# A graph network's last result tiles: the work of the last quarter's results put on other engines, with a region of its own for each tile

## The chip, the cores and the metric

The kernel runs on one core of one Trainium2 chip. The metric is the device time of an execution in microseconds. A core has five engines with instruction streams of their own: TensorE (PE; its weight loads are listed as PEld), VectorE (DVE), ScalarE (ACT), GpSimd (POOL) and SyncE (SP), which in this kernel mostly issues DMA transfers. They wait for each other on semaphores. SBUF is the memory of 128 partitions on the core, PSUM the memory that TensorE writes its products to.

## What is computed

Two layers on 3327 nodes with 256 features, each added to its input. Layer 0 does two steps of a normalised adjacency product beside a sparse attention of its own (not touched here). Layer 1 is a graph attention with four heads. Cut to what matters:

```python
h = jnp.maximum(_layernorm(x, axis=-1), 0.0)
x = x + layer0(h, adj, ...)              # below: x1; it ends in a layer norm, times ln_g, plus ln_b
h = jnp.maximum(_layernorm(x, axis=-1), 0.0)
x = x + layer1(h, adj, W, a)

def layer1(h, adj, W, a):
    hp = (h @ W).reshape(n, H, FH)       # H = 4 heads of FH = 64
    s = jnp.einsum('nhf,hf->hn', hp, a_src)
    d = jnp.einsum('nhf,hf->hn', hp, a_dst)
    e = jax.nn.leaky_relu(s[:, :, None] + d[:, None, :], ALPHA)
    e = jnp.where(adj[None, :, :] > 0, e, -jnp.inf)
    attn = jax.nn.softmax(e, axis=2)
    out = jnp.einsum('hij,jhf->ihf', attn, hp).reshape(n, H * FH)
    return jax.nn.elu(out)
```

With r for a row of `out`, elu(r) is max(r, 0) + min(exp(r), 1) - 1, so the result is max(r, 0) + min(exp(r), 1) + x1 - 1.

## The kernel before

All work is cut into pieces. `plan.put(engine, length, rank, fn, needs=..., take=..., give=..., lag=..., hold=...)` records one piece: `length` is the author's estimate of its duration, `rank` its priority, `needs` the pieces it comes after, `take` and `give` the buffers it uses up and gives back. `Plan.order` plays the pieces through with these estimates and so fixes the order in which each engine's instructions stand; what each instruction really waits for follows from the tiles that it reads and writes. A changed estimate or a new piece anywhere can therefore move instructions elsewhere.

The program's phases: a preparation, 26 row blocks of layer 0's step 0, 26 of step 1 (both with TensorE as the busiest engine), and layer 1's attention over the neighbours, `attend_neighbours`, in four quarters `b` of W = 832 columns of rows (the last one has 831 that count). In a quarter, for each of 26 blocks `j` of neighbours, SP loads two pieces of the adjacency matrix (`at`, L1570, four buffers), ACT makes a mask of them (L1580, L1581), DVE makes the masked exponents of four heads (`exponents`, L1592, from an operand `both`, which lies in the space of `qq` for quarters 0 and 2 and in that of `c` for 1 and 3, into one of four `e` buffers or three others), and TensorE multiplies (`product`, L1608; `sums`, L1622, the softmax's denominators). At a quarter's end ACT copies numerators and denominators from PSUM to a tile `ot` of the kind `e` (`leave`, L1668 and L1671).

Then come the quarter's results, in seven tiles of 128 rows (the last of 64, or 63 in the last quarter):

- `fetch` (SP, L1683): x1 of these rows from DRAM (`x1s`) to `f`, three buffers;
- `turn` (PE, L1689): three transposes into `px`, a PSUM tile with two buffers: two of numerators, one of denominators;
- `invert` (DVE, L1693): the reciprocals of four denominators, to `mv`;
- `elu` (ACT, L1701): for each of four heads Relu and Exp over 64 columns, with the reciprocal as scale, from `px` to `ystage`, two buffers; it gives `px` back;
- `add` (DVE, L1705, L1706): min(exp, 1) + relu, then - 1 + x1;
- `store` (SP, L1709): 128 KB to DRAM; it gives `ystage` back when it has landed.

In quarters 0 to 2 these pieces stand among the next quarter's work; in the last quarter nothing but a verdict follows. The verdict (L1785 to L1799: two transposes of one column, two reductions of 128 values, one operation to `again`) says whether a general version has to run after all; each engine reads `again` (L1806) and branches past that version.

Other lines that matter: `layer1_loads` (L717 to L720) loads `ln_g`, `ln_b` and weights into `late` in step 0; `add_b` (L1278, POOL) adds `ln_b` to x for each row in step 1, and the sum goes into x1, which `x1s` holds; `late["b"]` is used nowhere else. `step` (L923 to L953) is GpSimd's search for a threshold in layer 0.

Of the kernel before, what the change touches and what calls it, by code (L numbers as in the profile page):

```python
# [10 lines left out]
F32 = mybir.dt.float32  # L11
# [3 lines left out]
AF = mybir.ActivationFunctionType  # L15
ALU = mybir.AluOpType
# [3 lines left out]
P = 128  # L20
N = 3327
NT = 26
NP = NT * P
D = 256
DA = 64
H = 4
FH = 64
# [543 lines left out]
def fast(  # L571
# [17 lines left out]
    nc = tc.nc  # L589
    V, S, T, GP = nc.vector, nc.scalar, nc.tensor, nc.gpsimd  # L590
# [10 lines left out]
    x1s = spill.tile([NT, P, D], F32, name="x1s")  # L601
# [29 lines left out]
    with ExitStack() as l0:  # L631
        wpool = l0.enter_context(tc.tile_pool(name="wpool", bufs=1))
        small = l0.enter_context(tc.tile_pool(name="small", bufs=2))
        epool = l0.enter_context(tc.tile_pool(name="epool", bufs=4))
# [823 lines left out]
        def attend_neighbours(rows, ends, done, fulls):  # L1458


            W = NP // 4
# [4 lines left out]
            extra = {}  # L1466
# [25 lines left out]
            def spread_heads(t0, t1):  # L1492

                held = {}

                def turn():
                    held["ps"] = ps_x.tile([(t1 - t0) * H, P], F32, name="px")
                    T.transpose(held["ps"], sd[:, 0, t0:t1, :].rearrange("p t h -> p (t h)"), ident)

                def exps():  # L1500
                    held["rows"] = small.tile([7 * H, P], F32, name="rows", bufs=1)[: (t1 - t0) * H]
                    S.activation(held["rows"], held["ps"], AF.Exp, scale=1.0 - ALPHA)

                def store():
                    for t in range(t0, t1):
                        nc.sync.dma_start(
                            highs[:, t * P : (t + 1) * P], held["rows"][(t - t0) * H : (t - t0 + 1) * H, :]
                        )

                rank = min(30.0 + t1, 59.0)  # L1510
                a = plan.put("PE", 0.12, rank, turn, needs=[z[0] for z in ends[t0:t1]], take=["px"])
                a = plan.put("ACT", 0.3, rank, exps, needs=[a], take=["rows"], give=["px"])
                return plan.put("SP", 1.0, rank, store, needs=[a], give=["rows"], lag=3.0)
# [4 lines left out]
            def broadcast(b, rank):  # L1518
# [11 lines left out]
                    got.append(plan.put("SP", 0.1, rank, fetch, needs=[after], lag=7.0 + 5.0 * a))  # L1530
                return got

            used_heads = [None, None]
            evacuated = None
            both = broadcast(0, 59.5)
            for b in range(4):
# [140 lines left out]
                for x0 in range(0, W, P):  # L1677
                    m = min(P, W - x0, N - lo - x0)
                    held = {}

                    def fetch(m=m, at=lo + x0, held=held):
                        held["x1"] = small.tile([P, H * FH + 2 * H], F32, name="f", bufs=BUFS["f"])[:, :D]
                        nc.sync.dma_start(held["x1"][:m], x1s.rearrange("t p d -> (t p) d")[at : at + m, :])  # L1683

                    def turn(m=m, x0=x0, q=q, held=held):
                        held["pr"] = ps_x.tile([P, 3, P], F32, name="px")
                        ot = q["ot"].rearrange("p k c w -> p k (c w)")
                        for k in range(3):
                            T.transpose(held["pr"][:m, k, :], ot[:, k, x0 : x0 + m], ident)  # L1689

                    def invert(m=m, held=held):
                        held["rec"] = small.tile([P, 4], F32, name="mv", bufs=BUFS["mv"])
                        V.reciprocal(held["rec"][:m], held["pr"][:m, 2, ::32])  # L1693

                    def elu(m=m, held=held):
                        y = held["y"] = small.tile([P, 2, D], F32, name="ystage", bufs=BUFS["ystage"])
                        pr = held["pr"][:m, :2, :].rearrange("p a b -> p (a b)")
                        for k in range(H):
                            part = slice(k * FH, (k + 1) * FH)
                            for a, fn in enumerate((AF.Relu, AF.Exp)):  # L1700
                                S.activation(y[:m, a, part], pr[:, part], fn, scale=held["rec"][:m, k : k + 1])  # L1701

                    def add(m=m, held=held):
                        y = held["y"]
                        V.scalar_tensor_tensor(y[:m, 0], y[:m, 1], 1.0, y[:m, 0], ALU.min, ALU.add)  # L1705
                        V.scalar_tensor_tensor(y[:m, 0], y[:m, 0], -1.0, held["x1"][:m], ALU.add, ALU.add)  # L1706

                    def store(m=m, at=lo + x0, held=held):
                        nc.sync.dma_start(out[at : at + m, :], held["y"][:m, 0])  # L1709

                    touched = [ends[t][1] for t in range((lo + x0) // P, min(NT - 1, (lo + x0 + m - 1) // P) + 1)]
                    f_ = plan.put("SP", 0.1, r1, fetch, needs=[touched, [a for a, _ in ends]], take=["f"], lag=3.0)
                    a = plan.put(
                        "PE", 0.4, r1 + 0.02, turn, needs=[out_of], take=["px"], give=["e"] * (x0 + P >= W)
                    )
                    a = plan.put("DVE", 0.2, r1, invert, needs=[a], take=["mv"])
                    a = plan.put("ACT", 2.0, r1, elu, needs=[a], take=["ystage"], give=["px", "mv"])
                    a = plan.put("DVE", 1.0, r1, add, needs=[a, f_], give=["f"], hold=0.9)
                    plan.put("SP", 0.1, r1, store, needs=[a], give=["ystage"], lag=2.5)

# [13 lines left out]
        for n in range(STEPS):  # L1734
            base = 30.0 * n
            scaled = plan.put(
                "DVE", 0.2, base - 50.0,
                lambda: V.tensor_scalar(gk[:, : DA + 1], gk[:, : DA + 1], 1.0 / (NT // 2 * P), None, ALU.mult), needs=[sums],
            )
            cuts = (0, 3, NT // 2, NT)  # L1740
            of = {}
            for k in range(3):
                p = stats(cuts[k], cuts[k + 1], base + (-50.0, -2.35, 0.0)[k], [keys, fresh], scaled)
                of.update(dict.fromkeys(range(cuts[k], cuts[k + 1]), p))
            if n == 0:
                guessed[0] = [*{id(p): p for p in of.values()}.values()]
            rows = [Row(n, i) for i in range(NT)]
            found = [search(r, base + r.i, keys, of[r.i], fresh) for r in rows]
            if n == 0:
                drawn[0] = rows[-1].pieces["logits"]  # L1750
            fulls = [
                full(n, t, (min(1.0 + 1.15 * t, 27.0) if n == 0 else base + 1.0 + t), [p[0] for p in sources], [p[1] for p in sources] if n == 0 else loaded[0])
                for t in range(NT)
            ]
            done = [attention(r, base + r.i, *found[r.i], right) for r in rows]
            failed.append(plan.put("DVE", 2.2, base + NT, failures, n, needs=[[a for a, _ in found]]))
            if n == 0:
                ends = [finish1(r, done[r.i], base + r.i + 0.2) for r in rows]
                stored = [y for _, _, y in ends]
                fetched = plan.put(  # L1760
                    "SP", 0.3, base + NT, fetch_keys, needs=[drawn[0], [k for k, _, _ in ends[: LAST + 1]]], lag=5.0
                )
                keys, sums = [fetched] + [k for k, _, _ in ends], [g for _, g, _ in ends]

                right, after = [], [done, stored]
                for lo in range(0, NT, 4):
                    hi = min(lo + 4, NT)
                    right.append(plan.put("SP", 0.1, base + NT, fetch_rhs, lo, hi, needs=after, lag=7.0))
                    after = [plan.put("POOL", 0.02, -90.0, lambda: None, needs=right[-1:], lag=0.0)]
                fresh = failed + [r.pieces["guess"] for r in rows]  # L1770
                used, sources = sources, [(p,) for p in fulls]

                def layer1():
                    late["g"], late["b"], late["wa"], late["a"] = layer1_loads()

                a = plan.put("SP", 0.5, base + 4.0, layer1, needs=[used, done[3]], take=["et"], lag=8.0)
                layer1_ready = plan.put(
                    "DVE", 3.7, base + 5.0, lambda: layer1_scores(late["wa"], late["a"]), needs=[a], take=["et"],
                    give=["et", "et"],
                )  # L1780
            else:
                ends = [finish2(r, done[r.i], fulls[r.i], base + r.i + 0.2) for r in rows]
        attend_neighbours(rows, ends, done, fulls)
# [62 lines left out]
```

## Time and profile before

| | us |
|---|---|
| median of 3 runs | 2241.94 (2241.08 to 2243.65) |
| the profiled execution | 2240.52 |
| its span, first to last instruction | 2238.6 |
| PE busy | 2177.3 |
| DVE busy | 1615.0 |
| ACT busy | 1455.7 |
| POOL busy | 925.1 |

The span is what the profile divides; the profiled execution's own time is 1.9 us longer. Busy times of the engines overlap. In the stretch from 2216.5 to the end, 22.1 us, PE is busy for 5.4, ACT for 12.4, DVE for 7.6 and POOL for 0.

### The profile page before, as it was taken

The page shows a single profiled execution, that of the slowest core. Times are in us where ns is not written, and L with a number is a line of the kernel's source. Part 1 is how long each engine was busy: PE and PEld are TensorE (multiplying, and loading weights), DVE is VectorE, ACT ScalarE, POOL GpSimd, SP SyncE. Part 2 cuts the span into 40 slices and gives each one's busy share as a digit, 9 for nine tenths or more (in the row PEclk, how much of TensorE's full clock was granted, in tenths as well). Part 3 has the DMA queues.
Part 4 walks back from the last instruction along what each step waited for, and adds up shares of the span by engine and source line. Part 5 has one row for each costly group of instructions (what it writes and reads, how often), then busy time and mean ns, then how long its engine had stood idle before and what let it go on. Part 6 is the DMA issues. An engine that isn't in the chain of part 4 may idle for free.

```text
span 2238.6 us, 36037 instructions
## 1 busy us (share of the span) xinstructions
PE 2177.3 (97%) x11978; PEld 1537.8 (69%) x11978; DVE 1615.0 (72%) x4229; ACT 1455.7 (65%) x2795; POOL 925.1 (41%) x2214
## 2 busy tenths in 40 slices
PE   7999999999999999999999999999999999999997
PEld 5487778777887778877878887887887433333332
DVE  5576657546655744178979877888777998989895
ACT  5776686566566652478887877878774455464653
POOL 6455355435544541256656666566653200000000
PEclk9999999999999999999999999999999999999998
DMA  3012221212212222621212222222225344444341
GB/s 99 20 38 70 68 70 54 70 49 64 70 53 70 70 83 67 191 76 56 76 49 70 59 74 72 81 62 66 69 75 154 121 129 137 116 144 119 102 128 42
DMA packets 192036, 183.76 MB, mean 82 GB/s; under 512 B 15354, under 2 KB 146144, under 8 KB 191712
## 3 DMA queue, kind: packets, MB, share of 16 engines
q1 hardware_dynamic: 189856, 180.10, 27.6%
q8 instruction: 96, 1.57, 0.3%
q10 hardware_dynamic: 1984, 1.26, 0.2%
q14 instruction: 100, 0.82, 0.1%
HBM read 164.41 MB, written 15.94 MB: 81 GB/s over the span
## 4 chain that ended last, share of the span: by engine, by line
PE 75%; ACT 8%; POOL 6%; DVE 5%; issue 3%; DMA 1%; SPq 0%; ACTq 0%; POOLq 0%; DVEq 0%
PE acca L1042 20%; PE accf L1074 20%; PE pl L1608 12%; PE px L1030 6%; PE pl L856 6%; ACT junk L907 5%; PE acca L1622 3%; PE accf L1622 3%; PE px L1217 2%; POOL sc L920 1%; PE px L1312 1%; PE px L1169 1%; DVE cands L967 1%; DVE y L962 1%; ACT et L1035 1%
## 5 line engine op out<-in xcount | busy, mean ns | idle before, releaser
L1042 PE MATMUL acca<-rhs,et 128*128 128x256 f32 x2704 | 619.4, 380 | 1.0 <-ACT et L1035 0.9
L907 ACT ACTIVATE junk<-e,sc 128x3327 fp8e5<-128x3327 f32 x182 | 559.2, 3073 | 48.1 <-POOL sc L952 46.8
L1042 PEld LDWEIGHTS acca<-rhs,et 128*128 128x128 f32 x2704 | 499.9, 191 | 64.4 <-ACT et L1035 2.9
L1074 PE MATMUL accf<-c,at 128*128 128x256 f32 x1352 | 313.5, 382 | 5.5 <-ACT f L1081 5.5
L1074 PE MATMUL accf<-main,at 128*128 128x257 f32 x1352 | 312.0, 382 | 5.6 <-DMA at<-in_adjt_dram 5.3
L962 DVE SCALAR_TENSOR_TENSOR y<-e,sc 128x1664 f32<-128x1664 f32 x104 | 209.0, 2010 | 149.0 <-POOL sc L949 147.0
L1074 PEld LDWEIGHTS accf<-main,at 128*128 128x128 f32 x1352 | 252.8, 191 | 47.9 <-issue 6.5
L1074 PEld LDWEIGHTS accf<-c,at 128*128 128x128 f32 x1352 | 250.0, 190 | 47.7 <-ACT f L1081 10.3
L1035 ACT COPY et<-px 128x512 f32<-128x512 f32 (+1 forms) x364 | 192.7, 553 | 136.1 <-PE acca L1042 72.9
L967 DVE MAX8 cands<-y 128x8 f32<-128x208 f32 x832 | 242.6, 361 | 3.6
L1017 DVE SCALAR_TENSOR_TENSOR e<-e,thr 128x832 f32<-128x832 f32 x208 | 213.1, 1082 | 2.2 <-DVE thr L1012 0.5
L870 ACT ACTIVATE e<-pl 128x1024 f32<-128x1024 f32 x208 | 179.0, 864 | 37.7 <-PE pl L856 37.5
L1581 ACT ACTIVATE et<-at 128x448 bf16<-128x448 f32 (+1 forms) x204 | 112.2, 550 | 137.3 <-DVE e L1592 81.5
L1030 PE MATMUL px<-ident,e 128*128 128x128 f32 x1352 | 191.2, 275 | 9.2 <-DVE gk L766 4.5
L1030 PEld LDWEIGHTS px<-ident,e 128*128 128x128 f32 x1352 | 159.5, 141 | 51.8 <-issue 15.3
L1608 PE MATMUL pl<-e,main 128*64 128x416 f32 x1024 | 187.2, 515 | 0.0
L856 PE MATMUL pl<-kt,qq 64*128 64x512 f32 (+1 forms) x832 | 173.5, 535 | 0.0
L1608 PEld LDWEIGHTS pl<-e,main 128*64 128x64 f32 x1024 | 71.0, 137 | 107.3 <-issue 92.0
L1592 DVE SCALAR_TENSOR_TENSOR e<-c,low,et 128x832 f32<-128x832 f32 x128 | 128.6, 1072 | 8.2 <-PE accf L1622 3.9
L856 PEld LDWEIGHTS pl<-kt,qq 64*128 64x128 f32 x832 | 71.6, 186 | 82.1 <-issue 75.7
L1592 DVE SCALAR_TENSOR_TENSOR e<-qq,low,et 128x832 f32<-128x832 f32 x120 | 120.5, 1074 | 2.6 <-ACT e L1668 2.0
L1580 ACT ACTIVATE at<-at 128x448 f32<-128x448 f32 (+1 forms) x204 | 109.8, 538 | 11.9 <-DMA at<-in_adjt_dram 11.8
(507 smaller groups left out, 2987.3 us busy)
## 6 DMA issues: line engine op xcount, KB each, us to landing
at<-in_adjt_dram SPq DMA_DIRECT2D x414, 256.0 KB
at<-in_adjt_dram SPq DMA_DIRECT2D x102, 192.0 KB
at<-in_adjt_dram SPq DMA_DIRECT2D x52, 128.0 KB
ys<-ystage SPq DMA_DIRECT2D x26, 256.0 KB
rhs<-in_x_dram SPq DMA_DIRECT2D x26, 128.0 KB
ystage<-in_x_dram SPq DMA_DIRECT2D x26, 128.0 KB
base<-ys SPq DMA_DIRECT2D x26, 128.0 KB
x1s<-ystage SPq DMA_DIRECT2D x26, 128.0 KB
```

The lines of the kernel that those rows point to most:

```text
L856: T.matmul(pl[:, r, :m], qq[half, self.i, :], kt[half, 512 * k : 512 * k + m], start=True, stop=True,)
L870: S.activation(self.e[:, 1024 * k : 1024 * k + 2 * w].rearrange("p (r w) -> p r w", r=2), pl, AF.Exp, accum_out=(self.p0, self.p1, self.p2 ...
L907: S.activation(junk[:, :N], self.e[:, :N], fn, bias=t, scale=-1.0, accum_out=dst, saturate=False)
L962: V.scalar_tensor_tensor(self.y[:, : hi - lo], self.e[:, lo:hi], self.up, self.e[:, lo:hi], ALU.is_lt, ALU.mult, accum_out=(self.h0, self. ...
L967: V.max(self.cands[:, o // PIECE, :], self.y[:, o - lo : min(o + PIECE, hi) - lo])
L1017: V.scalar_tensor_tensor(piece, piece, self.thr[:, o : o + 1], piece, ALU.is_gt, ALU.mult)
L1030: T.transpose(pt[:, k, :], self.e[:, j * P : (j + 1) * P], ident)
L1035: S.copy(self.et[g][:, :m, :], self.pt.pop(g)[:, :m, :])
L1042: T.matmul(self.acc, et[:, j - 4 * g, :], rhs[self.n][:, j, :], start=(j == 0), stop=(j == NT - 1))
L1074: T.matmul(self.acc[:, : self.w], self.at[j // JC][:, j % JC, :], self.src[:, j, : self.w], start=(j == 0), stop=(j == NT - 1),)
L1592: V.scalar_tensor_tensor(held["e"][:, k, :], extra["both"][b % 2][:, k, :], low[:, j, k : k + 1], held["mask"], ALU.max, ALU.mult,)
L1608: T.matmul(q["acc"][a][k * FH : (k + 1) * FH, c, :C], main[:, j, h * FH : (h + 1) * FH], held["e"][:, h, c * C : (c + 1) * C], start=(j == 0),
```

## The change

The last quarter's results (b = 3) get pieces of their own; the other quarters keep theirs, but for one operation. Since all quarters share `x1s`, the "- 1" moves into it: `ln_b` becomes `ln_b - 1` once, by GpSimd, after it was loaded, so that `x1s` holds x1 - 1. (A layer norm of x1 - 1 is that of x1.)

- `fetch_all` (SP): x1 - 1 for four tiles at once into the space of `qq`, after quarter 2's last exponents (`used_heads[0]`), and for the other three into a buffer of the kind `e`, after the last quarter's last exponents. Each tile has 768 columns there: three parts of 256.
- `quotient` (DVE): the reciprocals, into columns of a tile `rows`, then one product of 256 columns from PSUM, with the reciprocal of each head repeated 64 times, to part 1. It gives `px` back.
- `parts` (ACT): Relu of part 1 to part 0, Exp of part 1 in place, 256 columns each.
- `add_x1` (POOL): part 2 (x1 - 1) plus part 0.
- `join` (DVE): min(part 1, 1) + part 2, to part 0.
- `store` (SP): as before, from part 0; no buffer is given back.

```diff
@@ spread_heads
-                    held["rows"] = small.tile([7 * H, P], F32, name="rows", bufs=1)[: (t1 - t0) * H]
+                    held["rows"] = small.tile([P, P], F32, name="rows", bufs=1)[: (t1 - t0) * H]
@@ attend_neighbours
+            last, f_ = {}, None
...
                     def add(m=m, held=held):
                         y = held["y"]
                         V.scalar_tensor_tensor(y[:m, 0], y[:m, 1], 1.0, y[:m, 0], ALU.min, ALU.add)
-                        V.scalar_tensor_tensor(y[:m, 0], y[:m, 0], -1.0, held["x1"][:m], ALU.add, ALU.add)
+                        V.tensor_add(y[:m, 0], y[:m, 0], held["x1"][:m])
+
+                    def fetch_all(x0=x0, lo=lo):
+                        if x0 == 0:
+                            last["rec"] = small.tile([P, P], F32, name="rows", bufs=1)
+                        y = extra["both"][0] if x0 == 0 else epool.tile([P, NP], F32, name="e").rearrange(
+                            "p (k w) -> p k w", k=4
+                        )
+                        for k in range(4):
+                            x = x0 + k * P
+                            n = min(P, W - x, N - lo - x)
+                            if n > 0:
+                                last[x] = y[:, k, : 3 * D].rearrange("p (a d) -> p a d", a=3)
+                                nc.sync.dma_start(
+                                    last[x][:n, 2], x1s.rearrange("t p d -> (t p) d")[lo + x : lo + x + n, :]
+                                )
+
+                    def quotient(m=m, held=held, x0=x0):
+                        y, held["rec"] = last[x0], last["rec"][:, x0 // P * H : (x0 // P + 1) * H]
+                        held["y"] = y
+                        V.reciprocal(held["rec"][:m], held["pr"][:m, 2, ::32])
+                        V.tensor_tensor(
+                            y[:m, 1].rearrange("p (h f) -> p h f", h=H),
+                            held["pr"][:m, :2, :].rearrange("p a (h f) -> p (a h) f", h=2),
+                            held["rec"][:m].unsqueeze(2).to_broadcast([m, H, FH]),
+                            ALU.mult,
+                        )
+
+                    def parts(m=m, held=held):
+                        y = held["y"]
+                        S.activation(y[:m, 0], y[:m, 1], AF.Relu)
+                        S.activation(y[:m, 1], y[:m, 1], AF.Exp)
+
+                    def add_x1(m=m, held=held):
+                        GP.tensor_add(held["y"][:m, 2], held["y"][:m, 2], held["y"][:m, 0])
+
+                    def join(m=m, held=held):
+                        y = held["y"]
+                        V.scalar_tensor_tensor(y[:m, 0], y[:m, 1], 1.0, y[:m, 2], ALU.min, ALU.add)
...
-                    f_ = plan.put("SP", 0.1, r1, fetch, needs=[touched, [a for a, _ in ends]], take=["f"], lag=3.0)
+                    if b < 3:
+                        f_ = plan.put("SP", 0.1, r1, fetch, needs=[touched, [a for a, _ in ends]], take=["f"], lag=3.0)
+                    elif x0 % (4 * P) == 0:
+                        f_ = plan.put("SP", 0.4, r1, fetch_all, needs=[used_heads[0] if x0 == 0 else [last_e, f_], touched], take=["e"] * (x0 > 0), lag=4.0)
                     a = plan.put(
                         "PE", 0.4, r1 + 0.02, turn, needs=[out_of], take=["px"], give=["e"] * (x0 + P >= W)
                     )
+                    if b == 3:
+                        a = plan.put("DVE", 0.65, r1, quotient, needs=[a, f_], give=["px"])
+                        a = plan.put("ACT", 0.8, r1, parts, needs=[a])
+                        z_ = plan.put("POOL", 0.8, r1, add_x1, needs=[a, f_])
+                        a = plan.put("DVE", 0.45, r1, join, needs=[z_], hold=0.4)
+                        plan.put("SP", 0.1, r1, store, needs=[a], lag=2.5)
+                        continue
@@ fast, step 0
                 def layer1():
                     late["g"], late["b"], late["wa"], late["a"] = layer1_loads()
+                    late["less"] = lambda: GP.tensor_scalar(late["b"], late["b"], -1.0, None, ALU.add)
...
+                less = plan.put("POOL", 0.6, base + 5.0, lambda: late["less"](), needs=[a])
...
+                layer1_ready = [layer1_ready, less]
```

## Prediction

> **What bounds the kernel now.** The page first: its engine table says that TensorE fills the span and that no other engine does.
>
> ```profile
> PE 2177.3 (97%) x11978; PEld 1537.8 (69%) x11978; DVE 1615.0 (72%) x4229; ACT 1455.7 (65%) x2795; POOL 925.1 (41%) x2214
> ```
>
> So work taken from ACT or DVE is worth nothing where TensorE is busy beside it. The 40 slices give PE 9 everywhere but at the start and in the last one. The end is therefore read by itself. The chain of waits, asked for 2216 us to the end, leaves TensorE at 2217.06:
>
> ```profile
> 2216.57 0.49 PE px L1689 x3
> 2217.06 0.02 issue
> 2217.08 0.19 DVE mv L1693
> 2217.28 0.02 issue
> 2217.30 1.75 ACT ystage L1701 x8
> 2219.05 0.02 issue
> 2219.08 0.43 DVE ystage L1705
> 2219.51 0.02 issue
> 2219.53 0.43 DVE ystage L1706
> 2219.97 0.02 issue
> 2219.99 0.02 SPq L1709
> 2220.00 0.03 issue
> 2220.03 1.73 DMA out_dram<-ystage
> ...
> 2233.13 0.42 DVE ystage L1706
> ```
>
> The columns are start, length, who. Seven result tiles run one after the other from 2217.06 to 2233.55: 16.5 us with TensorE nearly idle. A tile is a transpose, a reciprocal, eight ACT operations over 64 columns, two DVE additions and a store; because `ystage` has two buffers, ACT also waits for a store to land (1.73 us, twice). The groups of lines for the same stretch say that ACT is the engine of it:
>
> ```profile
> L1701 ACT ACTIVATE ystage<-px,mv 128x64 f32<-128x64 f32 (+1 forms) x56 | 11.8, 337 | 3.7 <-DMA out_dram<-ystage 2.3 <-DVE ystage L1706 1.2 <-DVE mv L1693 0.2
> ```
>
> Last, the line that reads the verdict (L1806) shows what stands after the last result:
>
> ```profile
> L1806 SPq TENSOR_LOAD <-again x1: 683/683/683, 2231.5 to 2231.5; - x1
> L1806 SPq COMPARE_BRANCH  x1: 50/50/50, 2234.0 to 2234.0; - x1
> L1806 SPq EVENT_SEMAPHORE  x8: 17/17/17, 2236.7 to 2237.2; - x8
> ```
>
> SP branches 0.46 us after the last addition, its next instruction comes 2.6 us later, and the closing waits end at 2238.6: 5.05 us behind the last addition. The verdict itself was read earlier, at 2231.5, beside ACT's work.
>
> **What the Trainium skill says.** "ScalarE: Activation LUTs", section "What ACT_TABLE_LOAD costs": an operation with immediate scale and bias takes 186 ns + 0.833 ns per column, each pointer operand adds about 93 ns. This trace agrees: L1580 (no pointer, 416 columns in the mean) takes 538 ns against 533. For 256 columns that is 0.40 us. "SBUF — State Buffer", section "SBUF: two separate sides": a DVE operation with two SBUF inputs and a GpSimd operation exclude each other, the later one is blocked. The trace agrees: at 143.7 the add L1225 (POOL, 0.72) started just ahead of a DVE L962, which then took 2.40 instead of 1.95; at 349.96 the add came second, took 2.03, and ended 0.59 after L962. So an add holds up a DVE operation by some 0.5 us. "TensorE: Matmul & The Clock Gate", section "What's actually happening": an idle array falls to half clock after some 3.4 us. The trace agrees: three transposes take 0.55 at 2220.73 and 0.90 at 2223.67.
>
> **The change, part by part.** Steps of the last quarter's seven tiles:
>
> *Removed:* 56 ACT operations, 11.8 us busy, and ACT's 2.3 us of waits for stores (every tile has its own region now). *In their place:* 14 ACT operations of 256 columns. L1580's 384 columns take 0.51 and 448 take 0.56 to 0.58, which makes 0.38 to 0.40 at 256; I take 0.39, so Relu and Exp with the wait between them are 0.81 a tile. Upper end: L1298, 256 columns with pointer operands, 0.60.
>
> *DVE:* a reciprocal (0.18, L1693), then the product out of PSUM with a broadcast operand, not in this trace. Nearest rows: L1323, the same product from SBUF, 0.42, and L1173, a copy out of PSUM of that size, 0.42. I take 0.45, bounds 0.42 and 0.50. It reads one operand from SBUF, so I let it not contend with GpSimd. The join is one operation of L1705's kind, 0.42, where two stood.
>
> *GpSimd:* the add of 128x256, 0.72 (L1225, L1278). Bounds: 0.72 alone, 1.3 each time it meets a join.
>
> *TensorE:* a tile waits for its `px` buffer, which is now given back by the product instead of by eight ACT operations: 0.53 a tile (0.90 cold). It falls behind other work, as DVE is slower.
>
> The built order of DVE is quotients 0 to 3, join 0, quotients 4 and 5, join 1, quotient 6 (with the first verdict reduction inside), joins 2 to 6, then the second verdict reduction and `again`. DVE alone: 7 x (0.18 + 0.03 + 0.45) + 7 x 0.42 + 0.28 = 7.84, less 0.08 at each of some 15 places where the next operation does not depend on the last one (L1705 follows L1706 after 0.34) = 6.6. Now the waits, walked through by hand with these durations: product 0 ends 2217.74, Relu 2218.17, Exp 2218.59, add 2218.94; tile 3: product 2219.56, Exp 2220.78, add 2221.49, join 2223.82; tile 6: product 2222.53, Exp 2223.38, add 2224.40, join 2225.45. DVE loses 0.1 for `px` and 1.6 at joins behind adds: 2217.08 + 6.6 + 1.7 = 2225.4. Without the port's exclusion the last join ends 2224.2; with cold transposes 2226.05; with adds of 1.0 everywhere 2226.3; with ACT at 0.60 2226.5; all of these together 2226.9.
>
> *The end:* `again` was ready at 2231.46, 1.7 us before the last addition began; now it stands behind the last join. Reduction and final operation take 0.4 (0.28 + 0.15, L1798 and L1799, the first overlapping), the read 0.69, register work and branch 0.4: SP branches 1.5 after the last join instead of 0.46. The rest, 2.63 + 1.9 us, is as before, so the end stands 6.1 behind the join instead of 5.05. The seven stores (0.35 each on SP) go out before, at the joins' pace.
>
> Span: 2225.45 + 6.1 = 2231.55, that is 7.05 less.
>
> *Moved and added elsewhere, costed at nothing:*
> - Loads of x1. Four go to the space of the exponents' first operand (`qq`) when quarter 2 has read it last. In SP's order they stand ahead of the `at` loads issued at 2083.09, 2084.06, 2087.07 and 2088.04, and wait for DVE until 2086.37. SP is then held from 2080.4 to 2086.4 and issues four loads (0.43 each, L1683): the next `at` load goes out at 2088.1, 5 us late, lands some 3 us later (an estimate: 128 KB, L1709, take 1.73, and this is 256 KB), and ACT wants it at 2098.18 (L1580). Margin 7 us. The last three wait for the `e` buffer of row 21, free at 2207.9, and have until 2221.
> - GpSimd's b - 1, 128x256, at most 0.72, in row 5 of step 0: it stands behind L953 (ends 223.37), and the next GpSimd instruction begins at 226.34 after 2.74 us of waiting for ACT. Its loads have landed at 219.2. Without that cover it would cost 0.7 in one row's search.
> - The planner's order moves two matmuls and one `at` load around 250 us past three small DMAs: that load goes out at 254.8 instead of 252.2, wanted at 259.9; beyond that margin TensorE would wait as long as it is late.
> - In quarters 0 to 2 an addition replaces L1706: 0.42 (L1090) for 0.42.
>
> **Time.** The profiled execution took 2240.52 with a span of 2238.6. 7.05 less is 2233.5 there; the median of the runs is 2241.94, so 2234.9.
>
> **Rivals.** *GpSimd becomes the bound of the end.* For it: seven adds of 0.72 and seven joins of 0.42 that exclude each other, and GpSimd's times are rough. If every add takes 1.3 plus 0.1 of wake-up, the last ends 2218.2 + 9.8 = 2228.0, the join 2228.5, the span 2234.6: 4.0 less, 2237.9. Against: only adds 3 to 6 meet joins. *The closing part grows.* All five engines now branch within 1 us of each other, where four did it 1.7 us ahead; TensorE's branch shows 3.39 already. With 2 us more: 5 less, 2236.9. *A larger gain:* port exclusion not felt, product at 0.42: 2233.5. *Slower:* SP's queue. The fetch of x1 is parked ahead of the `at` loads; if its wait ended not at 2086.4 but with the next DVE result that is counted, late masks would reach ACT, DVE and TensorE. From 2093 on each microsecond costs one, and from 2100 on it eats the whole gain; held until 2105, it makes 2247. Against: the operand's last reader is quarter 2's last exponent, ended at 2086.37. That the change doesn't do what it says is excluded by the built order.
>
> **How the numbers follow.** Forecast 0.76, a larger gain 0.04, the closing part 0.08 (all three faster), GpSimd as the bound 0.09 (inside 0.2%), SP 0.03 (slower). 0.2% is 4.5 us, so "same" is 2237.5 to 2246.4. The likeliest one's own bounds, 2224.2 to 2226.9 for the last join, are 2233.7 to 2236.4; the three runs lie 2.6 us apart, so some 0.8 on each side, and upward to part of the rivals: 2233.0 to 2237.3.
>
> **What would show it.** In the profile after: last join at 2225 to 2226; ACT's two operations 0.39 each; adds of 0.72 for tiles 0 to 2 and over 1 later; joins of 0.42 to 0.9; SP's branch 1.5 behind the last join; no change in TensorE's time of entering the transposes (2216.5). Wrong would be: transposes later than 2217.5 (a cost in the quarters), or products above 0.6.

## The result, and the profile after

| us | before | after | repeat of after |
|---|---|---|---|
| median (range), runs | 2241.11 (2239.72 to 2243.65), 8 | 2235.27 (2233.45 to 2236.41), 8 | 2234.09 (2232.20 to 2235.23), 5 |
| ratio to before, 95% interval | | 0.9974 (0.9965 to 0.9983) | 0.9964 (0.9951 to 0.9978) |
| span of the profiled execution | 2238.6 | 2234.2 | 2233.1 |
| TensorE enters the last transposes | 2216.5 | 2218.7 | 2217.3 |
| from there to the end of the last result on DVE | 17.05 | 8.56 | 8.56 |
| from there to the end of the span | 5.07 | 6.96 | 7.20 |

The kernel became faster, by 5.8 us in the runs made right after the prediction and by 7.15 in the repeat (each against before timed beside it, hence the two ratios). The last two rows are called the join time and the end part below; together they are "the tail": 22.1 before, 15.5 and 15.8 after. The tail is the better measure of the change than the time: TensorE's entry into it differs by 1.4 us between two traces of before and by 1.3 between two of after.

The chain of waits after, from the first result on (columns: start, length, who):

```profile
2220.41 0.73 POOL qq L1742
2221.14 0.02 issue
2221.16 0.73 POOL qq L1742
...
2222.72 0.69 POOL qq L1742
2223.41 0.02 issue
2223.43 0.74 POOL e L1742
2224.16 0.11 issue
2224.27 1.66 POOL e L1742
...
2226.81 0.41 DVE e L1746
2227.22 0.21 DVE verdict L1852
2227.43 0.02 issue
2227.45 0.15 DVE again L1853
```

ACT, which carried this chain before, is gone from it. GpSimd's additions stand in its place, one behind the other with at most 0.11 us between them, and `again` stands last. The groups of lines of the same stretch, by shape (columns: tiles and shapes, count, busy us, mean ns, idle before):

```profile
L1742 POOL TENSOR_TENSOR qq<-qq 128x256 f32<-128x256 f32 x4 | 3.0, 756 | 453.7 <-ACT qq L1738 453.7
L1742 POOL TENSOR_TENSOR e<-e 128x256 f32<-128x256 f32 x2 | 2.5, 1266 | 0.0
L1746 DVE SCALAR_TENSOR_TENSOR qq<-qq 128x256 f32<-128x256 f32 x4 | 1.8, 459 | 0.0
L1729 DVE TENSOR_TENSOR qq<-px,rows 128x256 f32<-128x256 f32 x4 | 1.7, 424 | 0.1
L1739 ACT ACTIVATE qq<-qq 128x256 f32<-128x256 f32 x4 | 1.7, 417 | 0.1
L1738 ACT ACTIVATE qq<-qq 128x256 f32<-128x256 f32 x4 | 1.6, 405 | 0.6 <-DVE qq L1729 0.6
```

The wide operations cost what their nearest rows gave. The additions of the tiles in `e` don't: 1.27 in the mean of two, one of them 1.65. The line that reads the verdict shows the rest. Before, the four engines that the prediction doesn't show branched so (columns: count, shortest, median and longest in ns, first and last start):

```profile
L1806 ACTq COMPARE_BRANCH  x1: 54/54/54, 2232.2 to 2232.2; - x1
L1806 POOLq COMPARE_BRANCH  x1: 45/45/45, 2232.3 to 2232.3; - x1
L1806 PEldq COMPARE_BRANCH  x1: 3390/3390/3390, 2232.3 to 2232.3; - x1
L1806 DVEq COMPARE_BRANCH  x1: 76/76/76, 2233.8 to 2233.8; - x1
```

After:

```profile
L1860 SPq EVENT_SEMAPHORE  x8: 17/17/17, 2232.3 to 2232.8; - x8
...
L1860 SPq TENSOR_LOAD <-again x1: 784/784/784, 2227.7 to 2227.7; - x1
L1860 ACTq COMPARE_BRANCH  x1: 54/54/54, 2228.2 to 2228.2; - x1
L1860 POOLq COMPARE_BRANCH  x1: 45/45/45, 2228.2 to 2228.2; - x1
L1860 PEldq COMPARE_BRANCH  x1: 3427/3427/3427, 2228.3 to 2228.3; - x1
L1860 DVEq COMPARE_BRANCH  x1: 76/76/76, 2228.3 to 2228.3; - x1
...
L1860 SPq COMPARE_BRANCH  x1: 50/50/50, 2228.9 to 2228.9; - x1
```

The last join ended at 2227.22. SP branches 1.65 behind it (0.46 before), and its next instruction comes 3.38 later (2.68 before). All five engines branch within 0.7 us, where ACT, POOL and PE were 1.7 us ahead of SP before.

### The profile page after: what moved, and what is told of

The parts are those of the page before. It is cut to its first block, busy times and chain, and to the rows that moved or that the text cites. A ratio compares the mean times of both kernels' runs of the same rounds, so it can differ in the third digit from the quotient of the medians.

```text
span 2234.2 us, 35999 instructions
## 1 busy us (share of the span) xinstructions
PE 2177.5 (97%) x11978; PEld 1538.1 (69%) x11978; DVE 1614.5 (72%) x4229; ACT 1449.4 (65%) x2753; POOL 931.5 (42%) x2222
## 3 DMA queue, kind: packets, MB, share of 16 engines
q8 instruction: 96, 1.57, 0.3%
## 4 chain that ended last, share of the span: by engine, by line
PE 69%; issue 9%; ACT 9%; POOL 6%; DVE 5%; DMA 2%; SPq 0%; POOLq 0%; DVEq 0%; ACTq 0%
PE acca L1042 20%; PE accf L1074 19%; PE pl L1609 9%; ACT junk L907 6%; PE px L1030 6%; PE pl L856 5%; PE acca L1623 2%; PE accf L1623 2%; PE px L1217 2%; POOL sc L920 1%; PE px L1312 1%; ACT et L1035 1%; DVE cands L967 1%; DVE y L962 1%; PE px L1169 1%
```

## The experiments

Each kernel was timed in five rounds, the repeat of before once. A ratio is to the kernel before, timed beside it. Entry is the start of the first of the last quarter's transposes. "Step" is the time from SP's branch to its next instruction; the end part is branch, step and a last 1.92 (2.8 to 2.9 in the two runs with DVE additions).

| run | median, ratio (95%) | entry | join time | end part: branch behind last result, step | tail |
|---|---|---|---|---|---|
| before | 2241.11 | 2216.50 | 17.05 | 5.07: 0.46, 2.68 | 22.11 |
| before_again | 2242.24, one run | 2217.91 | 17.07 | 5.36: 0.46, 2.97 | 22.43 |
| before_late | 2243.68, 1.0005 (0.9996 to 1.0013) | 2216.68 | 17.07 | 6.89: 1.57, 3.40 | 23.96 |
| after | 2235.27, 0.9974 (0.9965 to 0.9983) | 2218.66 | 8.56 | 6.96: 1.65, 3.38 | 15.52 |
| after_again | 2234.09, 0.9964 (0.9951 to 0.9978) | 2217.33 | 8.56 | 7.20: 1.66, 3.62 | 15.76 |
| no_less | 2235.15, 0.9969 (0.9957 to 0.9982) | 2217.91 | 8.57 | 7.26: 1.63, 3.71 | 15.83 |
| regions | 2237.97, 0.9983 (0.9977 to 0.9990) | 2217.92 | 13.18 | 5.83: 0.76, 3.14 | 19.01 |
| no_add | 2233.63, 0.9958 (0.9944 to 0.9972) | 2218.73 | 7.66 | 6.89: 1.54, 3.42 | 14.54 |
| dve_add | 2238.20, 0.9979 (0.9970 to 0.9988) | 2216.79 | 12.28 | 6.18: 0.43, 2.85 | 18.47 |
| dve_add2 | 2237.47, 0.9975 (0.9964 to 0.9986) | 2218.52 | 10.79 | 6.08: 0.54, 2.76 | 16.87 |
| early_verdict | 2234.88, 0.9967 (0.9954 to 0.9979) | 2220.81 | 8.34 | 7.07: 1.67, 3.47 | 15.41 |
| mix5 | 2234.46, 0.9965 (0.9951 to 0.9978) | 2216.11 | 8.75 | 6.88: 1.48, 3.47 | 15.62 |
| early_mix5 | 2234.88, 0.9969 (0.9956 to 0.9981) | 2217.24 | 8.67 | 5.79: 0.74, 3.13 | 14.46 |
| early_split | 2234.40, 0.9962 (0.9948 to 0.9975) | 2219.86 | 8.68 | 5.35: 0.23, 3.20 | 14.03 |

### Is the late entry a cost of the change?

Two kernels were run unchanged a second time, and one without the b - 1:

> The kernel before once more, for a second trace. In the two profiled executions TensorE entered the last quarter's transposes at 2216.50 before and at 2218.66 after, 1.4 us of that already there at 50 us. Theory (chance of an execution, the change costs nothing up to the last quarter): this trace enters anywhere from 2216 to 2219, the tail from there to the end takes 22.1 again. Rival (the change costs 0.7 us or more early): it enters at 2216.5 to 2217, as before.

> The changed kernel once more. Theory (chance of an execution): TensorE enters the transposes between 2216 and 2219, nearer to 2217.5, and the tail from there to the end takes 15.5 again; time 2235.3 within 0.8. Rival (the change costs 0.7 us or more early): it enters at 2218 or later again.

```diff
-                less = plan.put("POOL", 0.6, base + 5.0, lambda: late["less"](), needs=[a])
...
-                layer1_ready = [layer1_ready, less]
```

> The changed kernel without GpSimd's b - 1 (the output is too large by 1 everywhere), so the order of the work around 250 us is that of before again. Theory (b - 1 and the order are hidden): 2235.3 within 0.6, no difference from the changed kernel. Rival (they delay step 0): 0.7 to 1.4 us less, 2233.9 to 2234.6.

Before entered at 2217.91 the second time and after at 2217.33: the order of the two is reversed. Without the b - 1 the entry is 2217.91, the time the same within its interval. The entry alone would say little, since it holds the chances of the whole execution. The stretch from 150 to 401 us, in which the b - 1 and the reordered work lie, can be compared by itself (from one ACT operation, at 149.87 in before, to another at 400.97): it took 250.97 and 250.96 in the two traces of after, 250.93 in no_less, and 251.10, 250.93 and 250.93 in before, before_again and before_late. So the b - 1 and the reordering cost less than 0.05 us there, though GpSimd took 0.89 for the operation, not 0.72. The last quarter itself can be read to 0.01 us, from one quarter's first copy of the numerators to the next (timeline of ACT; start, length, then the instruction). Of before:

```profile
2093.43 0.85 ACT L1668 COPY e<-pl 128x832 f32<-128x832 f32 x1 [5.42 <-PE pl L1608]
...
2212.29 0.85 ACT L1668 COPY e<-pl 128x832 f32<-128x832 f32 x1 [17.37 <-PE pl L1608]
```

and of after:

```profile
2095.59 0.85 ACT L1669 COPY e<-pl 128x832 f32<-128x832 f32 x1 [5.42 <-PE pl L1609]
...
2214.45 0.85 ACT L1669 COPY e<-pl 128x832 f32<-128x832 f32 x1 [17.37 <-PE pl L1609]
```

118.86 in both, with equal waits: x1's loads parked in SP's queue are free, in this quarter where they would have to show. The difference in entry arises before. Of the 2.16 us between the first traces of the two kernels 1.44 were there at 30 us (a copy on ACT at 29.85 and 31.29), long ahead of the b - 1 at 224.7, and 2.15 at 901 us. Later the stretch from some 1656 to 1856 us takes either 198.5 to 198.8 or 200.1 to 200.2, without a pattern by kernel that I could find: the two traces of before and before_late have the short value, eleven of the changed kernel and its variants have it six times and the long one five times. Whether the change makes the long one likelier isn't settled by so few.

### What part is due to the regions alone?

```diff
                     def quotient(m=m, held=held, x0=x0):
...
                         V.reciprocal(held["rec"][:m], held["pr"][:m, 2, ::32])
-                        V.tensor_tensor(
-                            y[:m, 1].rearrange("p (h f) -> p h f", h=H),
-                            held["pr"][:m, :2, :].rearrange("p a (h f) -> p (a h) f", h=2),
-                            held["rec"][:m].unsqueeze(2).to_broadcast([m, H, FH]),
-                            ALU.mult,
-                        )
...
                     def parts(m=m, held=held):
...
-                        S.activation(y[:m, 0], y[:m, 1], AF.Relu)
-                        S.activation(y[:m, 1], y[:m, 1], AF.Exp)
+                        pr = held["pr"][:m, :2, :].rearrange("p a b -> p (a b)")
+                        for k in range(H):
+                            part = slice(k * FH, (k + 1) * FH)
+                            for s, fn in enumerate((AF.Relu, AF.Exp)):
+                                S.activation(y[:m, s, part], pr[:, part], fn, scale=held["rec"][:m, k : k + 1])
...
                     def join(m=m, held=held):
...
-                        V.scalar_tensor_tensor(y[:m, 0], y[:m, 1], 1.0, y[:m, 2], ALU.min, ALU.add)
+                        V.scalar_tensor_tensor(y[:m, 0], y[:m, 1], 1.0, y[:m, 0], ALU.min, ALU.add)
+                        V.tensor_add(y[:m, 0], y[:m, 0], y[:m, 2])
...
```

GpSimd's piece goes, `parts` gives `px` back again, and the planner's lengths follow.

> The changed kernel with the arithmetic of before in the last quarter: eight ACT operations of 64 columns per tile with the reciprocal as scale, and two DVE additions; the regions of their own, the early load of x1 and b - 1 stay. Theory (the wide operations are most of the gain, the regions only end the waits for stores): last addition some 14 us behind TensorE's last product, 2.2 to 2.8 us less than before, 2238.3 to 2238.9. Rival (the waits for stores and buffers were most of it): 5 us less, 2236.

The join time fell from 17.05 to 13.18, by 3.9, the tail by 3.1. That is above the theory's 2.8 and far from the rival's 5. ACT's groups (tiles, count, busy us, mean ns, idle before) show why it is more than the 2.3 us of waits for stores:

```profile
L1736 ACT ACTIVATE qq<-px,rows 128x64 f32<-128x64 f32 x32 | 6.6, 425 | 0.2 <-DVE rows L1728 0.2
L1736 ACT ACTIVATE e<-px,rows 128x64 f32<-128x64 f32 x16 | 3.6, 618 | 0.0
L1736 ACT ACTIVATE e<-px,rows 63x64 f32<-63x64 f32 x8 | 1.8, 409 | 0.0
```

The idle time is 0.2 where it was 3.7. With two buffers, ACT had also waited 1.2 us for DVE's addition (L1706, in the row of before that the prediction shows), and that went too. ACT's busy time didn't change (12.0 against 11.8), so it is the bound again, at 13.2. The wide operations take the join time from there to 8.56: 4.6 more. They give back 1.1 to 1.4 in the end part, as `again` is then no longer hidden. Of the tail's 6.6 us the regions thus make 3.1 and the wide operations 3.5: about half each, where the theory had most of it in the wide operations.

### Does GpSimd set the last join?

```diff
-                        V.scalar_tensor_tensor(y[:m, 0], y[:m, 1], 1.0, y[:m, 2], ALU.min, ALU.add)
+                        V.scalar_tensor_tensor(y[:m, 0], y[:m, 1], 1.0, y[:m, 0], ALU.min, ALU.add)
...
-                        z_ = plan.put("POOL", 0.8, r1, add_x1, needs=[a, f_])
-                        a = plan.put("DVE", 0.45, r1, join, needs=[z_], hold=0.4)
+                        a = plan.put("DVE", 0.45, r1, join, needs=[a, f_], hold=0.4)
```

> The changed kernel without GpSimd's addition of x1 - 1 (the join adds Relu and Exp alone; x1 is still loaded), so that no GpSimd work is left in the last quarter. Theory (GpSimd's additions, back to back from the first Relu and held up by joins, set the last join): DVE's own sum of 6.6 plus 0.3 of waits remains, the last join ends 7.4 behind TensorE's entry into the transposes instead of 8.6, time 1.1 less than the changed kernel, 2233.7. Rival (DVE's sum sets it and GpSimd rides beside it): 0.3 less at most, 2234.5.

The join time is 7.66, 0.90 less than with the additions (1.1 and 0.3 were expected), and the tail 1.0 less. In that trace DVE runs nearly without a gap from the first reciprocal to the last join. So GpSimd's additions do set the end, but DVE stands only 0.9 us behind them. (The planner changed DVE's order with them: both reductions of the verdict now stand ahead of the last join, so the 0.9 is a net value. In after itself DVE loses 1.3 to the additions: 0.62 of waiting and 0.72 by which three joins are longer than 0.41.) How the two meet (timeline of after; the number before the engine is the length of all xN together):

```profile
2223.43 3.17 POOL L1742 TENSOR_TENSOR e<-e 128x256 f32<-128x256 f32 x3
...
2224.26 0.74 DVE L1746 SCALAR_TENSOR_TENSOR qq<-qq 128x256 f32<-128x256 f32 x2
2224.93 0.40 DVE L1746 SCALAR_TENSOR_TENSOR e<-e 128x256 f32<-128x256 f32 x1
...
2225.96 1.26 DVE L1746 SCALAR_TENSOR_TENSOR e<-e 128x256 f32<-128x256 f32 x2 [0.62 <-POOL e L1742]
```

Of the three additions in `e` the second began, by the chain, at 2224.27, where a join had begun at 2224.26; three joins ran, to 2225.33, and it ended at 2225.93, 0.60 after them. That is the exclusion which the Trainium skill describes ("SBUF — State Buffer", section "SBUF: two separate sides"), and the trace agrees: the later of the two waits, and here for three DVE operations in a row. DVE then waited 0.62 for it.

The same addition on DVE, first as the planner ordered it, then with the quotients ahead:

```diff
-                        GP.tensor_add(held["y"][:m, 2], held["y"][:m, 2], held["y"][:m, 0])
+                        V.tensor_add(held["y"][:m, 2], held["y"][:m, 2], held["y"][:m, 0])
...
-                        z_ = plan.put("POOL", 0.8, r1, add_x1, needs=[a, f_])
+                        z_ = plan.put("DVE", 0.42, r1, add_x1, needs=[a, f_])
```

> The changed kernel with the addition of x1 - 1 on DVE instead of GpSimd. Theory (an addition of 0.42 more per tile on DVE, and no port to share): DVE's sum grows by 7 x 0.36 = 2.5 from 6.6 to 9.1 and the waits go, the last join ends 9.6 to 9.9 behind the entry, time 1.0 to 1.3 more, 2236.0. Rival (the additions on GpSimd cost more through the shared port than on DVE): no more than the changed kernel, 2234.8 or less.

It missed: 12.28 instead of 9.6 to 9.9. The planner had put later tiles' quotients behind earlier tiles' additions and joins, and the last tile's quotient began only at 2227.2, 10.4 behind the entry, with its whole chain still to come. So this run says nothing of what an addition costs.

```diff
-                        a = plan.put("DVE", 0.65, r1, quotient, needs=[a, f_], give=["px"])
+                        a = plan.put("DVE", 0.65, r1 - 0.5, quotient, needs=[a, f_], give=["px"])
```

> The changed kernel with the addition of x1 - 1 on DVE, as in the first run of that kind, whose order of work put four joins ahead of the fourth to seventh quotient; here the quotients go first, as in the changed kernel. Theory (a DVE addition is worth 0.34 to 0.42 a tile): DVE works back to back, 7.1 (the sum without additions, as measured) + 7 x 0.34 = 9.5 and 0.56 for the first transposes, last join 10.0 behind the entry instead of 8.6, 1.5 more. Rival (the shared port costs as much as the additions): last join 8.6 to 9.0 behind the entry.

The join time is 10.79, 3.1 above that without additions: 0.45 for each of seven, not 0.34. In the first of these two traces a dependent pair of addition and join takes 0.87 (starts at 2219.27, 2219.80 and, the next addition, 2220.14), so the join starts 0.53 after the addition, where one that depends on nothing would follow after 0.34. In the second trace the last four additions stand so, directly ahead of their joins (0.86 to 0.87 from one to the next), the first three do not: 4 x 0.53 + 3 x 0.34 = 3.1. GpSimd's additions cost 0.9 in all, DVE's 3.1: the move to GpSimd is worth 2.2 us of join time in this order, port and all. If all seven stood apart from their joins it would be 1.5 (an estimate: 7 x 0.34 less 0.9). Of the tail it is 1.1 to 1.4, as the flag is hidden again in the run with DVE's additions, and the times, 0.9975 against 0.9974 and 0.9964, don't tell the two apart.

### Why did the end part grow?

Two theories were put to the test with the kernel before, whose flag was tied to the last addition:

```diff
+                        final["y"] = y
...
-        V.tensor_tensor(again, verdict[:, 0:1], verdict[:, 1:2], ALU.max)
+        V.tensor_tensor(verdict[:, 0:1], verdict[:, 0:1], verdict[:, 1:2], ALU.max)
+        V.scalar_tensor_tensor(again, final["y"][:1, 0, :1], 0.0, verdict[:, 0:1], ALU.mult, ALU.max)
```

> The kernel before with its flag made to depend on the last addition (times zero), and nothing else moved: all five engines then wait for the last addition and branch together, as in the changed kernel, but with the old work ahead. Theory (the end part grew because the flag stands behind the last result and all engines branch together): SP's branch 1.4 to 1.6 behind the last addition instead of 0.46, SP's next instruction 3.4 to 3.7 later instead of 2.7 to 3.0, end part 6.8 to 7.2 instead of 5.05 to 5.4, time 1.7 more than before. Rival (the second term comes from the stores, which the changed kernel issues closer together): the branch moves by 1.0, but the step after it stays at 2.7 to 3.0, time 1.0 more.

```profile
L1809 SPq EVENT_SEMAPHORE  x8: 17/17/17, 2238.7 to 2239.3; - x8
L1809 SPq TENSOR_LOAD <-again x1: 771/771/771, 2234.2 to 2234.2; - x1
...
L1809 SPq COMPARE_BRANCH  x1: 50/50/50, 2235.3 to 2235.3; - x1
```

From the last addition, which ended at 2233.7, SP's branch stands 1.57, its step is 3.40, the end part 6.89: the changed kernel's end part, made in the old kernel by moving one value. Stores that come close together are not needed for it. (The time rose by 1.2 us against the median of before timed beside it, 2242.46; the interval holds both no change and the 1.7 expected.) The growth by 1.9 is thus two terms, both brought about by the flag behind the last result: 1.1 to 1.2 until SP's branch, and 0.4 to 1.0 for a longer step (3.40 here and 3.38 to 3.71 in after, after_again and no_less, against 2.68 and 2.97). That the step is longer because all five engines branch at once is not shown. It fits these runs, but in regions they branch within 0.8 us too, and the step is 3.14.

The cure that suggests itself is an early flag. The verdict's two transposes, its reductions and `again` went into the last quarter, at its blocks 18 to 22 of 26:

```diff
                     def exponents(a, j=j, held=held, b=b):
+                        if a == 0 and b == 3:
+                            {18: judge, 22: lambda: (reduce(0), reduce(1))}.get(j, lambda: None)()
...
                     def product(a, j=j, held=held, q=q, open_acc=open_acc, b=b):
+                        if a == 0 and b == 3 and j == 20:
+                            across(0), across(1)
```

> The changed kernel with the verdict (five DVE operations, two transposes, two reductions) moved to the middle of the last quarter, so that the flag is ready long before the last join, as nothing in the results changes it. Theory (standing behind the last join it costs 1.1 on SP's way to the branch, and 0.8 in the branches, which all five engines take together): SP's branch 0.5 behind the last join instead of 1.6, closing part 5.0 instead of 7.0, time 1.7 less with 0.3 lost on TensorE for the moved transposes, 2233.1. Rival (the closing part has grown because the last join comes early against something else, such as the stores): the branch comes earlier but SP's next instruction doesn't, 0.3 less at most.

The end part stayed at 7.07. The rival had that, but with an earlier branch, and SP's branch came no earlier behind the last join. SP's stores tell why (columns as for the verdict's line above):

```profile
L1770 SPq DMA_DIRECT2D out_dram<-qq x4: 332/346/1050, 2224.4 to 2227.7; - x4
L1770 SPq DMA_DIRECT2D out_dram<-e x3: 382/615/798, 2228.8 to 2230.0; - x3
```

With the flag ready, PE, POOL and ACT branch when their own work ends, at 2225.7 to 2227.6, while SP has four stores to issue. These took 1.05, 0.62, 0.38 and 0.80 instead of 0.31 to 0.40 each in after, and SP came to its branch 1.67 behind the last join, as late as with the late flag. The step is another matter:

```profile
L1867 SPq EVENT_SEMAPHORE  x8: 17/17/17, 2234.3 to 2234.8; - x8
...
L1867 DVEq COMPARE_BRANCH  x1: 76/76/76, 2228.9 to 2228.9; - x1
...
L1867 SPq COMPARE_BRANCH  x1: 50/50/50, 2230.8 to 2230.8; - x1
```

DVE branches 2.0 us ahead of SP, the other three 3.2 to 5.2, and still the step is 3.47. This speaks against the theory that engines which branch together are what makes it long; the cause stays open. The quarter also became 0.46 longer (119.32 between the copies), the price of the moved verdict; 0.3 was expected.

Then the last two tiles lost Relu and GpSimd, with and without the early verdict (`exp_only` puts Exp of part 1 into part 0, `add_here` is the last line, the join takes parts 0 and 2):

```diff
+                        if x0 >= 5 * P:
+                            b_ = plan.put("ACT", 0.4, r1, exp_only, needs=[a])
+                            a = plan.put("DVE", 0.42, r1, add_here, needs=[a, f_], hold=0.4)
+                            a = plan.put("DVE", 0.42, r1, join, needs=[a, b_], hold=0.4)
...
+                        V.scalar_tensor_tensor(y[:m, 2], y[:m, 1], 0.0, y[:m, 2], ALU.max, ALU.add)
```

> As with the early verdict, and the last two tiles take ACT's Exp alone, with max(z, 0) + x1 - 1 in one DVE operation in place of Relu and GpSimd's addition; GpSimd adds for tiles 0 to 4. Theory (GpSimd's chain sets the last join): five additions end by 2223.0 to 2223.5 counted from an entry of 2217.3, DVE's sum is 6.6 + 0.84 = 7.4 with 0.3 of waits, last join 8.0 behind the entry instead of 8.6; with the early verdict 2232.5, the fastest. Rival (DVE's sum is already the bound): last join 9 behind the entry, 2233.5.

> The changed kernel with the last two tiles' x1 - 1 added on DVE together with max(z, 0) (no Relu on ACT, no GpSimd there), verdict where the changed kernel has it. With the early verdict this one took 14.5 from the entry to the end, the changed kernel 15.5 to 15.8, the early verdict alone 15.4. Theory (the mix moves the last join by nothing, 8.6 to 8.8, as DVE is full; the gain came from the flag being ready and SP's stores being through before the other engines branch): 15.5 to 15.9. Rival (the mix itself shortens the end): 14.5 to 15.

The join time is 8.67 with the early verdict and 8.75 without, not below 8.56: here the rival of early_mix5 (9) was nearer than its theory (8.0), DVE is full. The end part is 6.88 with the late flag and 5.79 with the early one. So the mix is worth nothing by itself; with it the stores are spread differently (two of 0.51, the rest as ever), and the early flag pays in the tail. In the time it doesn't show: 0.9969 against 0.9965 without the early flag. That the mix's own work has no part in this is shown by mix5; that the slowed stores are what differs is read from the traces, not tested alone.

```diff
-                        plan.put("SP", 0.1, r1, store, needs=[a], lag=2.5)
+                        plan.put("ACT" if x0 == 4 * P else "SP", 0.1, r1, store, needs=[a], lag=2.5)
...
-                        nc.sync.dma_start(out[at : at + m, :], held["y"][:m, 0])
+                        (nc.scalar if b == 3 and x0 == 4 * P else nc.sync).dma_start(out[at : at + m, :], held["y"][:m, 0])
```

> Early verdict and the last two tiles on DVE as before, and the store of the tile that is joined last is issued by ACT instead of SP. Theory (SP's branch waits for its own store issues, 0.74 behind the last join with one or two of them slowed to 0.5): SP has one store less, its branch comes 0.3 to 0.5 behind the last join, 14.1 to 14.4 from the entry to the end. Rival (ACT's branch, now also behind the last join, makes the end later): 14.6 or more.

SP's branch stands 0.23 behind the last join, and the tail is 14.03, the shortest of all and 1.5 to 1.7 below the changed kernel's. The quarter costs 0.46 more, so some 1.0 to 1.3 should remain; the ratio, 0.9962, can't be told from the changed kernel's 0.9964 and 0.9974. It is the fastest by its tail, not shown to be so by the time.

## Why the prediction was right

The forecast, 2234.9, is met (2235.27, and 2234.09 in the repeat). As a gain it was 7.05; measured are 5.8 and, in the repeat, 7.15, while the tail, free of the chances ahead of it, lost 6.6. Its two halves are met less well: the last join came 0.4 sooner behind the entry, the end 0.9 to 1.1 later behind the join.

- *Entry unchanged:* right for the quarters, to 0.01 us. The sign that was named against it (transposes later than 2217.5) did appear in the first trace, and was a spread of executions that one trace of before could not show.
- *ACT's operations 0.39, product 0.45, join 0.42:* measured 0.41, 0.42, and 0.41 for a join alone; joins beside an addition took 0.48, 0.54 and 0.93.
- *Additions 0.72 for the first tiles, over 1 when they meet joins, at most 1.3:* in order 0.73, 0.73, 0.84, 0.73, 0.88, 1.65 and 0.71 (63 rows). The upper bound was too low, since it let an addition meet one join, not three in a row.
- *DVE's sum 6.6 and waits of 1.7, last join 8.95 behind the entry:* 8.56. In after's own trace DVE waits 0.16 for `px` (0.1 forecast), and the additions cost it 0.62 of waiting and 0.72 in longer joins (1.34, where the walk by hand had 1.6). With 0.58 until the first reciprocal that leaves 6.5 for the sum. Both terms were right to 0.2 us.
- *End part 6.1:* 6.96 and 7.20. This is the term that was mis-sized. Of its two steps the first, SP's branch 1.5 behind the last join, measured 1.65. The second, "the rest, 2.63 + 1.9 us, is as before", was wrong by 0.7 to 1.0: the step grew to 3.4 to 3.6. The rival "the closing part grows" foresaw this with 2 us as its price and a chance of 0.08; before_late shows that a late flag makes the step longer, by 0.4 to 0.7. Its reason, that all five branch together, isn't shown. (It also has four engines branching 1.7 us ahead of SP before; there were three, DVE was 0.25 ahead.)
- *GpSimd becomes the bound:* it is in the chain of waits, yet the last join came 0.4 earlier behind the entry than forecast, where the rival had it 3.05 later: additions 0 to 4 meet few joins.
- *SP's parked loads, the b - 1, the reordering:* nothing, as forecast. The next mask begins on ACT at 2100.34, 2098.18 before, which is the offset of 2.16 between the two traces.

Of the 8.49 us that the join time lost (8.1 forecast), 1.9 went into the end part (1.05 forecast). The sum, 6.6, is 0.45 below the forecast's 7.05, because the two errors partly cancel. That the first median lies 0.4 from the forecast is in part luck besides: in two sets of runs the gain over before differs by 1.3.

## What to carry to other kernels

Work that stands hidden beside the last results comes into the open when these get faster: price every instruction behind the last one anew, flags and branches too. Before a bottleneck is moved to a new engine, look how far behind the next one stands (here DVE, 0.9 us), as that is all that a further improvement of the new bound can bring. And where the entry into a stage varies by more than the difference looked for (here 1.3 to 1.4 us, against 0.9 for the additions), compare the stage from its own first instruction and leave the total to many runs.

## What the runs showed of the hardware

- After its branch past the general version SP's next instruction came 2.7 to 3.0 us later in four traces (before, before_again, dve_add, dve_add2), 3.1 to 3.2 in three (regions, early_mix5, early_split) and 3.4 to 3.7 in seven. In six of these seven all five engines branch within 0.9 us; early_verdict (3.47, the others 2.0 to 5.2 ahead) and regions (3.14, within 0.8) don't fit that. What sets it is open.
- An SP instruction that issues a store takes 0.31 to 0.40 in the tail of after. In three runs whose flag was ready before the last stores, one that began 1.6 to 2.0 us after another engine's branch took 0.77 (early_split), 1.05 (early_verdict) and 1.20 (dve_add2). The distance alone does not decide it: at 2.0 one took 0.51 (early_mix5), at 1.7 one took 0.35 (dve_add). Whether the fetching of instructions behind a branch is what slows it was not tested.
- A GpSimd addition of 128x256 that starts beside a run of DVE operations with two SBUF operands waits for the whole run: 1.65 us for 0.73 of work, with three joins (1.64 to 1.65 in after, after_again and no_less).
- The same tile less a constant (one operand, one immediate) took GpSimd 0.89, longer than the sum of two tiles, 0.73. It took 0.89 to 0.90 in all ten traces that have it, with no DVE operation beside it.
